# Cross-attention with a layer norm on one core: another order of all engines from the third tile on, and another ending for tiles 48 to 55

## The chip, the core and the metric

The kernel runs on one core of one Trainium2 chip. A core has a TensorE (PE in the profile) for matrix products, a VectorE (DVE), a ScalarE (ACT) and a GpSimd (POOL) for the rest, and a SyncE (SP) that issues most of the DMA transfers. Each engine runs its own instructions in order and waits on semaphores for the others. Matrix products are written to PSUM, eight banks of 128 x 512 floats; everything else lies in SBUF.

The metric is the device time of one execution, in microseconds. The times before are those of three runs.

## What is computed

Four sequences of 2048 rows attend to contexts of 77 rows, 512 features, 16 heads of 32. The projection is followed by a residual and a layer norm, everything in 32 bits:

```python
B, S, D, H = (2, 1024, 512, 16)
HD = D // H
qs = (q @ wq).reshape(Bq, Lq, H, HD).transpose(0, 2, 1, 3)
ks_ = (k @ wk).reshape(Bq, Lk, H, HD).transpose(0, 2, 1, 3)
vs = (v @ wv).reshape(Bq, Lk, H, HD).transpose(0, 2, 1, 3)
scores = jnp.einsum('bhqd,bhkd->bhqk', qs, ks_) / jnp.sqrt(jnp.float32(HD))
scores = jnp.where(mask[:, None, :, :], -jnp.inf, scores)
attn_w = jax.nn.softmax(scores, axis=-1)
attn = jnp.einsum('bhqk,bhkd->bhqd', attn_w, vs)
attn = attn.transpose(0, 2, 1, 3).reshape(Bq, Lq, H * HD)
out = attn @ wo + q
mu = jnp.mean(out, axis=-1, keepdims=True)
var = jnp.mean((out - mu) ** 2, axis=-1, keepdims=True)
return (out - mu) / jnp.sqrt(var + EPS) * gamma + beta
```

Here `q` is `x` (4 x 2048 x 512), and `k` and `v` are the context (4 x 77 x 512).

## The kernel before

The 8192 rows are 64 tiles of 128 rows. Two tiles make a pair (32 pairs, written b), four make a group (16 groups) for the query projection. A product of 32-bit numbers is made of three products of rounded parts: each operand is split into a high part and the rest (`xth` and `xtl`, `wqh` and `wql`, `AH` and `AL`, `woh` and `wol`).

The whole program is one string, `ORDER` (L49 to L143). Each of its words is one step: a letter for the kind, a number for the tile, pair or group, and sometimes a part. The loop at the end of `xattn_layernorm` issues the steps in the order of the string, and since a step's instructions go to the engine that its function names, the string sets the order in which each engine runs its work. A second table, `SLOTS`, says for every buffer of a kind, in the order in which they are asked for, which of the places it gets: `mm` for the eight banks of PSUM, `PT` and `B` for two buffers each, `o` for eight, and so on. A step waits until the place that it writes is free.

The steps of a tile t of pair b, with the letter that stands for each in `ORDER`:

- Query: `g` loads four features' blocks of `x` transposed (SP), `i` rounds them (ScalarE, L265), `j` takes the rest (GpSimd, L269), `Q` makes one of four query blocks of a group with 12 matmuls (L275), `q` copies it out of PSUM (VectorE, L289).
- Scores: `S`, 64 short matmuls into four banks (L399). `T` with a part 0 to 3 adds the mask, takes the row maxima of four heads and writes to one of three `pbuf` (VectorE, L416). `e` with a part is the exponential of four heads, with its sum (ScalarE, L431). `r` is the reciprocal of the sums (VectorE, L441), `n` the normalisation (GpSimd, L446); the last tile does both in halves, `h` and `m` (L452, L458).
- Regrouping: `t` transposes blocks of 32 x 32 (VectorE, L467) into `B`; twelve DMAs per pair, `P` (L478; `U` for the two tiles of the last pair), move the blocks into `PT`. Their last letter is the queue: `s` for SP, `a` for ScalarE, `g` for GpSimd.
- Values' product: `V` for a pair (32 matmuls, L492), `W` for a tile of the last pair. `a` and `b` (`c` and `d` there) round the result (ScalarE, L521) and take the rest (VectorE, L525).
- Output: `O` projects with 12 matmuls (L548). The residual is added in one of two ways. With `X`, TensorE puts `x` into the bank first, by a product with an identity matrix in 32 bits (L537), and `O` adds to it. Without it, `+` adds the rows of `x` on VectorE (L557). `x` is the load of those rows (L533).
- Ending: `s` takes the moments (VectorE, L568 and L569, or L596 and L598). Then there are two ways. In the first, for a pair, `v` makes the inverse deviation and the shift with four small instructions (GpSimd, L574 to L577), `k` scales (ScalarE, L583), `f` multiplies by gamma and adds beta (GpSimd, L587 and L588). In the second, for a single tile, `u` makes the inverse deviation with two small instructions (GpSimd, L602 and L603), `y` takes off the mean and multiplies by gamma (VectorE, L614), `z` multiplies by the inverse deviation and adds beta (VectorE, L617). `w` stores (SP, L591).

Before, tiles 0 to 47 end in the first way and tiles 48 to 63 in the second, and `LATE = 48` tells `s` which moments a tile needs. Eight tiles have their residual on TensorE: 49, 51, 54, 55, 57, 59, 62 and 63.

One wait is set by hand. Where the word behind `S` among TensorE's words is a `V`, the first matmul of the scores also waits for the twelve regroupings of that `V` (`early_waits`, L385).

The middle of the string repeats, pair after pair, on TensorE: scores of the even tile, the values' product of two pairs back, scores of the odd tile, two query blocks, two output tiles.

Of the kernel before, what the change touches and what calls it, by code (L numbers as in the profile page):

```python
# [8 lines left out]
F32 = mybir.dt.float32  # L9
# [8 lines left out]
P = 128  # L18
# [25 lines left out]
LATE = 48  # L44
# [4 lines left out]
ORDER = """  # L49
R1 R0 R3 E l0 l2 C2 C0 C1 C3 g5 M4.4 A0 M0.1 M12.4 A1 M1.3 A3 M8.4 K2 A2 H2 J3 p i3 g4 J1 K0 i2 S0 I2 j2 S1 T0.1  # L50
e0.1 T0.2 H0 T0.0 j3 e0.0 T1.0 T0.3 e0.2 T1.1 Q4 T1.2 e0.3 F0 T1.3 I0 e1.2 r0 n0 S2 q4 e1.0 S3 T2.3 T2.0 Q7 i5 T2.1
e1.3 F2 j5 T2.2 t0 e1.1 Q6 i4 F1 g7 r1 Y1 e2.0 F3 L1 n1 T3.2 Q5 x1 T3.1 e2.1 q6 T3.3 e3.3 j4 t1 B0 e3.2 T3.0 P0.4s
q7 x2 e2.3 q5 P0.7s S4 D0 P0.5s e3.0 S6 P0.10s T4.3 P0.0s G0 B2 e3.1 R2 T4.0 g6 P0.2s e4.3 r3 P0.8s G3 n3 P0.11s B1
e2.2 D2 P0.6s T4.1 T4.2 e4.1 G2 r2 Q8 i7 t3 x11 n2 P0.3s e4.2 P0.9s T6.0 P0.1s T6.2 e4.0 j7 x0 Q9 T6.3 Z13.s t2
e6.0 Z0.s G1 e6.3 S5 r4 P1.0s T6.1 n4 P1.7s q8 Q10 e6.2 T5.3 P1.6s T5.0 P1.10s e6.1 T5.2 P1.3s T5.1 P1.5s i6 S7 t4
P1.1s Z1.s e5.3 Q11 j6 P1.11s T7.2 P1.9s e7.2 T7.3 Z2.s q9 P1.8s r6 e7.3 D1 Q13 n6 P1.4s T7.0 P1.2s T7.1 e7.0 g9
q10 x3 e7.1 Z12.s V0 q13 g8 q11 Z11.s a0.0 r7 e5.0 t6 V1 Z10.s n7 Z7.s e5.1 b0.0 S9 N t7 a1.1 Q12 e5.2 b1.1 P3.9s
a1.0 P3.5s r5 T9.0 n5 P3.11s e9.0 Q14 b1.0 P3.3s T9.2 Z8.s e9.2 T9.1 P3.2s T9.3 P3.4s e9.3 t5 Y0 S8 P3.10s a0.1 O2
P3.7s q12 i9 T8.1 P3.0s T8.0 e9.1 P2.3s T8.3 P3.8s q14 Z9.s e8.0 O3 T8.2 P3.1s b0.1 P3.6s e8.3 +2 Z5.s r9 P2.0s n9
e8.2 S10 +3 P2.7s S11 P2.2s T10.0 e8.1 s2 P2.9s O1 j9 s3 T10.3 e10.3 r8 T10.1 v1 g10 Q15 +1 e10.1 Z4.s t9 n8 P2.6s  # L60
k2 x6 T10.2 P2.11s e10.0 V3 f2 t8 i8 T11.3 P4.11s O0 e11.3 T11.2 P2.4s j8 q15 P4.9s a3.0 T11.0 P2.8s k3 T11.1 P2.1s
a3.1 S12 w2 e10.2 M16.4 P2.5s b3.1 Q19 +0 P4.6s e11.1 r10 P4.5s T12.2 n10 P2.10s b3.0 e11.2 T12.0 P4.10s O6 s0
P4.7s i10 f3 P4.8s s1 P4.0s e11.0 q19 T12.3 S13 e12.2 t10 v0 w3 V2 P4.3s r11 x7 T13.2 a2.0 n11 e13.2 P4.1s T13.1 O7
# [110 lines left out]
def xattn_layernorm(  # L174
# [381 lines left out]
    def residual(t):  # L556
        nc.vector.tensor_tensor(od[t], pos.pop(t), od[t], ALU.add)  # L557
# [202 lines left out]
```

## Time and profile before

| What | us |
| --- | --- |
| Runs shown | 524.79, 529.14, 530.62 |
| Median of them | 529.14 |
| Span of the profiled execution | 525.7 |
| TensorE's clock granted in it, of full speed | 0.997 |

The profiled execution has no time of its own beside its span, which is from its first instruction to its last; it lies inside the runs' spread. The profile counts an engine as busy from the start to the end of each instruction. TensorE's matmuls overlap, so that a matmul of 512 columns is shown as some 0.39 us long while the next starts 0.23 us later; the time of a group of them is therefore read from the chain of work, which counts from start to start. A row of the groups of instructions has the line, the engine, the operation, what it writes and reads by the program's names, the form, the count, then the busy time in us and the mean of one in ns, and then the idle time ahead of them with what ended it. "issue" is time in which the engine waited for nothing that the profile shows.

### The profile page before, as it was taken

How to read it: one execution, taken by the hardware profiler on the slowest of the kernel's cores; microseconds unless marked ns; L12 is line 12 of the kernel's file. 1: busy time of each engine (PE TensorE's matmuls, PEld its weight loads, DVE VectorE, ACT ScalarE, POOL GpSimd, SP SyncE). 2: the span in 40 equal slices, each digit the busy share in tenths (PEclk: the TensorE clock that was granted, in tenths of full speed). 3: DMA queues.
4: the chain of work that ended last, by engine and by line, in shares of the span. 5: the costliest groups of instructions: out<-in, count | busy, mean ns of one | idle time of the engine just before them, and what ended most of it. 6: DMA issues, size and time to landing. Idle time of an engine off the chain costs nothing.

```text
span 525.7 us, 20274 instructions
## 1 busy us (share of the span) xinstructions
PE 507.2 (96%) x6845; PEld 388.8 (74%) x6845; DVE 476.0 (91%) x2572; ACT 460.4 (88%) x2215; POOL 405.5 (77%) x371
## 2 busy tenths in 40 slices
PE   9999999999989999999999999999999999999994
PEld 6987777778767777777777777767777777767662
DVE  5798988989979989998989989998998999999997
ACT  6699999998989999999999999999999999987400
POOL 2475736889889889969989887988888689869551
PEclk9999999999999999999999999999999999999998
DMA  8948577785797677988887687797868987388555
GB/s 300 401 125 241 148 205 196 195 236 147 205 243 226 189 197 225 217 219 219 215 225 207 178 224 226 184 254 195 213 190 225 259 251 189 91 219 218 158 176 199
DMA packets 59261, 110.85 MB, mean 211 GB/s; under 512 B 9430, under 2 KB 11758, under 8 KB 59158
## 3 DMA queue, kind: packets, MB, share of 16 engines
q1 hardware_dynamic: 55702, 102.75, 69.1%
q0 software_dynamic: 2496, 5.77, 3.9%
q10 hardware_dynamic: 960, 1.05, 0.8%
q8 instruction: 54, 0.88, 0.7%
q14 instruction: 49, 0.40, 0.3%
HBM read 41.79 MB, written 16.78 MB: 111 GB/s over the span
## 4 chain that ended last, share of the span: by engine, by line
PE 51%; DVE 12%; DMA 10%; POOL 9%; SPq 9%; ACT 5%; issue 3%; POOLq 0%; DVEq 0%
PE pq L275 20%; PE po L548 15%; PE sc L399 7%; SPq L478 6%; PE pa L492 6%; DMA PT<-B 6%; ACT pbuf L431 4%; POOL o L587 3%; DVE B L467 3%; POOL o L588 2%; POOL pbuf L446 2%; DVE pbuf L416 2%; PE pv L326 2%; DMA stage_a<-xT 1%; POOL xtl L269 1%
## 5 line engine op out<-in xcount | busy, mean ns | idle before, releaser
L431 ACT ACTIVATE pbuf<-pbuf,nm 128x77 f32<-128x77 f32 x1024 | 352.7, 350 | 16.2 <-DVE nm L416 13.4
L431 ACT ACTIVATION_READ_ACCUMULATOR pbuf<-pbuf,nm 128x1 f32 x1024 | 194.6, 190 | 0.0
L416 DVE CUSTOM_DVE_ANT_0 pbuf<-sc,mb 128x77 f32<-128x77 f32 x1024 | 170.2, 231 | 9.6 <-PE sc L399 8.5
L446 POOL TENSOR_TENSOR pbuf<-pbuf,ri 128x1232 f32<-128x1232 f32 x63 | 142.8, 2267 | 39.4 <-DVE ri L441 23.6
L467 DVE STREAM_TRANSPOSE B<-pbuf 128x1280 f32<-128x1280 f32 x64 | 96.1, 1502 | 9.8 <-POOL pbuf L446 5.4
L548 PE MATMUL po<-woh,AH 128*128 128x512 f32 x256 | 102.6, 401 | 0.0
L548 PE MATMUL po<-woh,AL 128*128 128x512 f32 x256 | 100.1, 391 | 2.3 <-DVE AL L525 2.3
L275 PE MATMUL pq<-xth,wqh 128*128 128x512 f32 (+1 forms) x256 | 101.8, 398 | 0.2
L548 PE MATMUL po<-wol,AH 128*128 128x512 f32 x256 | 99.8, 390 | 0.0
L275 PE MATMUL pq<-xtl,wqh 128*128 128x512 f32 (+1 forms) x256 | 98.3, 384 | 0.0
L275 PE MATMUL pq<-xth,wql 128*128 128x512 f32 (+1 forms) x256 | 98.1, 383 | 0.0
L416 DVE DVE_READ_ACCUMULATOR2_ANT nm<- 128x1 f32 x1024 | 83.9, 82 | 0.0
L399 PEld LDWEIGHTS sc<-kct,q 32*64 32x64 f32 x4096 | 52.8, 130 | 32.9 <-issue 17.1
L587 POOL TENSOR_TENSOR o<-o,gam 128x512 f32<-128x512 f32 x48 | 62.5, 1302 | 13.7 <-ACT o L583 13.4
L269 POOL TENSOR_TENSOR xtl<-xtf,xth 128x1024 fp32r<-128x1024 f32 x28 | 67.3, 2403 | 6.7 <-ACT xth L265 6.6
L399 PE MATMUL sc<-kct,q 32*64 32x77 f32 x4096 | 63.6, 238 | 8.4 <-issue 3.8
L588 POOL TENSOR_TENSOR o<-o,bet 128x512 f32<-128x512 f32 x48 | 62.4, 1300 | 3.8
L492 PE MATMUL pa<-PT,vsb 96*32 96x256 f32 x992 | 59.9, 382 | 0.0
L521 ACT CAST AH<-pa 128x512 fp32r<-128x512 f32 x64 | 36.4, 572 | 25.0 <-DVE st L596 10.6
L548 PEld LDWEIGHTS po<-woh,AL 128*128 128x128 f32 x256 | 48.0, 188 | 13.8 <-DVE AL L525 3.5
L548 PEld LDWEIGHTS po<-woh,AH 128*128 128x128 f32 x256 | 48.0, 188 | 13.7 <-issue 2.0
L275 PEld LDWEIGHTS pq<-xth,wqh 128*128 128x128 f32 x256 | 48.1, 188 | 12.0 <-PE sc L399 0.5
(108 smaller groups left out, 666.0 us busy)
## 6 DMA issues: line engine op xcount, KB each, us to landing
PT<-B SPq DMA_DIRECT2D x343, 128.0 KB
xtf<-xT SPq DMA_DIRECT2D x28, 512.0 KB
o<-x SPq DMA_DIRECT2D x56, 256.0 KB
out<-o SPq DMA_DIRECT2D x56, 256.0 KB
PT<-B POOLq DMA_DIRECT2D x25, 128.0 KB, 3.8
xtf<-xT SPq DMA_DIRECT2D x4, 256.0 KB
stage_a<-wq SPq DMA_DIRECT2D x4, 256.0 KB
stage_a<-wk SPq DMA_DIRECT2D x4, 256.0 KB
```

The source lines that it names most:

```text
L269: nc.gpsimd.tensor_tensor(l[:, c : c + 2], fx.pop((g, c)), xh[g][:, c : c + 2].bitcast(F32), ALU.subtract)
L275: nc.tensor.matmul(pq, w[:, c, m * P : (m + 1) * P], r[g][:, c, rs], start=(n == 0), stop=(n == 11))
L399: mm = nc.tensor.matmul(sc[j][r0 : r0 + SR, g * NK : (g + 1) * NK], qs[q, g, rs.start + r0 : rs.start + r0 + SR], kct[q, g, t // TPB, keys ...
L416: nc.vector.tensor_tensor_reduce(pb[:, h // 2, (h % 2) * NK : (h % 2 + 1) * NK], scs[t][j][:, g * NK : (g + 1) * NK], mb[:, t % TPB, keys_ ...
L431: nc.scalar.activation(pb[:, h // 2, (h % 2) * NK : (h % 2 + 1) * NK], pb[:, h // 2, (h % 2) * NK : (h % 2 + 1) * NK], AF.Exp, bias=nmax[t ...
L446: nc.gpsimd.tensor_tensor(pv, pv, rv.to_broadcast((P, NP, 2, NK)), ALU.mult)
L467: nc.vector.transpose(bt.rearrange("p c q r -> p q c r"), pbuf[t % NPB].rearrange("p q (c r) -> p q c r", c=5),)
L492: nc.tensor.matmul(pas[b, g // 2][HD * j : HD * (j + 1), (g % 2) * BLK : (g % 2 + 1) * BLK], vsb[:, 2 * b // TPB, h % 2, HD * (h // 2) : H ...
L521: nc.scalar.copy(*at_part(once(ahs, b, [P, NG, BLK], F32R, "AH"), b, i, by_tile))
L548: nc.tensor.matmul(pos[t], a[:, c, rs], w[:, c, :], start=(first and c == 0 and n == 0), stop=(c == NC_D - 1 and n == 2),)
L587: nc.gpsimd.tensor_tensor(o, o, gam, ALU.mult)
L588: nc.gpsimd.tensor_tensor(o, o, bet, ALU.add)
```

## The change

From the third tile on (behind the step `S5`) `ORDER` is another string, and the places of the banks and of the buffers `xtf`, `PT`, `AH`, `AL`, `o`, `mv` and `rn` follow it. Functions, formats and the number of places stay. Two things besides the order change:

- Pairs 24 to 27 (tiles 48 to 55) end in the first way: `v`, `k` and `f` take the place of `u`, `y` and `z`. Tiles 56 to 63 keep the second. Instead of `LATE`, a set `ALONE` is read off the string.
- Tiles 49, 51, 54, 55, 57 and 59 have their residual on VectorE, `+`, instead of `X`. Tiles 62 and 63 keep `X`.

Counted over the string, `X` goes from 8 words to 2, `+` from 56 to 62, `u`, `y` and `z` from 16 to 8 each, `v` from 24 to 28, `k` and `f` from 48 to 56 each. All other kinds of step keep their number.

The diff, with a few lines of the two strings from the place where they part (behind `S5`; the lines are also broken elsewhere) and from their ends:

```diff
-LATE = 48
 LAST = 56
...
-e6.0 Z0.s G1 e6.3 S5 r4 P1.0s T6.1 n4 P1.7s q8 Q10 e6.2 T5.3 P1.6s T5.0 P1.10s e6.1 T5.2 P1.3s T5.1 P1.5s i6 S7 t4
-P1.1s Z1.s e5.3 Q11 j6 P1.11s T7.2 P1.9s e7.2 T7.3 Z2.s q9 P1.8s r6 e7.3 D1 Q13 n6 P1.4s T7.0 P1.2s T7.1 e7.0 g9
...
+T4.1 T4.2 e4.1 G2 r2 Q8 i7 t3 x11 n2 P0.3s e4.2 P0.9s T6.0 P0.1s T6.2 e4.0 j7 x0 Q9 T6.3 Z13.s t2 e6.0 Z0.s G1 e6.3 S5
+Z12.s D1 q8 e6.2 i6 r4 T6.1 e6.1 Z2.s T5.0 e5.0 P1.3s P1.4s T5.1 Z11.s P1.7s q9 P1.6s P1.2s Q11 n4 t4 P1.0s S7 T7.1
+e7.2 e7.0 Q12 n6 t6 e5.3 r7 n7 S9 T9.2 e9.2 q12 r5 n5 T9.3 Z1.s V0 Y0 Z3.s g9 g8 T9.0 t7 P3.7s P3.5s P3.2s P3.4s V1
...
-U63.9a u59 y59 d62 z59 O62 z60 z57 z58 +61 z56 W63 s62 w56 c63 w51 X63 s61 u62 w57 d63 O63 u61 w58 y62 z55 y61 w55
-z62 z61 s63 w61 w59 u63 y63 w62 z63 w60 w63
+U62.3a U62.0a U62.4a W62 U63.1a y59 u58 v27 k55 k47 f53 U63.2s U63.11s W63 w53 y58 z57 w57 k54 f54 w54 +60 s60 z56 u60
+z59 z58 w58 w56 f55 w55 w59 c62 d62 O62 +61 s61 y60 u61 c63 d63 s62 u62 z60 y61 w60 w52 z61 w61 f47 w47 O63 s63 u63
+y62 z62 y63 w62 z63 w63
 """
+
+ALONE = {int(w[1:]) for w in ORDER.split() if w[0] in "u@"}
...
-        mvs[t, 1] = tiny.tile([P, 4], F32, tag="mvt", bufs=64 - LATE, name=f"mvt_{t}")
+        mvs[t, 1] = tiny.tile([P, 4], F32, tag="mvt", bufs=len(ALONE), name=f"mvt_{t}")
...
-        "+": lambda k, part: residual(k), "s": lambda k, part: (moments_one if k >= LATE else moments)(k),
+        "+": lambda k, part: residual(k), "s": lambda k, part: (moments_one if k in ALONE else moments)(k),
```

Three places show how the engines' rows move. In them a name carries the tile, pair or group and a buffer's number: `sc_38_3` is the fourth bank of tile 38's scores, `pa_16_0` half of pair 16's values' product, `PT_16` its regrouped weights, `po_31` the output of tile 31, `mvt_60` the moments of tile 60 and `o_55` the rows of tile 55.

The first place is TensorE around the values' product of pair 16, which reads the regrouped weights of tiles 32 and 33. Before, it stands between the scores of tiles 38 and 39:

```order
L399 MATMUL sc_38_2_5338<-kct_74,q_9_4717 64x77
L399 MATMUL sc_38_3_5339<-kct_74,q_9_4717 64x77
L492 MATMUL pa_16_0_5374<-PT_16_5047,vsb_75 32x256 x8
L492 MATMUL pa_16_1_5375<-PT_16_5047,vsb_75 32x256 x8
L399 MATMUL sc_39_0_5418<-kct_74,q_9_4717 64x77
L399 MATMUL sc_39_1_5419<-kct_74,q_9_4717 64x77
```

Now, the scores of tiles 39 and 40 stand ahead of it and an output of tile 31 behind it:

```order
L398 MATMUL sc_40_2_5489<-kct_74,q_10_5200 64x77
L398 MATMUL sc_40_3_5490<-kct_74,q_10_5200 64x77
L491 MATMUL pa_16_0_5523<-PT_16_4969,vsb_75 32x256 x8
L491 MATMUL pa_16_1_5524<-PT_16_4969,vsb_75 32x256 x8
L547 MATMUL po_31_5579<-woh_72,AH_15_5326 128x512
L547 MATMUL po_31_5579<-wol_73,AH_15_5326 128x512
```

So the product of pair 16 has moved back by two groups of scores, and the scores that also wait for its regroupings are those of tile 40 instead of 38.

The second place is SP's queue in the regrouping of pair 16. Before, its twelve transfers stand among two loads of rows, one of the transposed input and two stores:

```order
L478 DMA PT_16_5047<-B_16_4920 32x2x512
L533 DMA o_33_5051<-x 128x512
L262 DMA xtf_11_0_5056<-xT 128x1024
L478 DMA PT_16_5047<-B_16_4920 32x2x512 x2
L591 DMA out<-o_27_4239 128x512
L478 DMA PT_16_5047<-B_16_4920 32x2x512
L591 DMA out<-o_24_4167 128x512
L478 DMA PT_16_5047<-B_16_4920 32x2x512 x7
L533 DMA o_32_5253<-x 128x512
L478 DMA PT_16_5047<-B_16_4920 32x2x512
```

Now, there is one store among them, and the mask of the last sequence (a line's number is one less in the changed kernel):

```order
L477 DMA PT_16_4969<-B_16_4824 32x2x512 x4
L261 DMA xtf_11_0_4996<-xT 128x1024
L590 DMA out<-o_22_4216 128x512
L477 DMA PT_16_4969<-B_16_4824 32x2x512
L375 DMA m8_3_5012<-mask 128x1536
L477 DMA PT_16_4969<-B_16_4824 32x2x512
L532 DMA o_28_5093<-x 128x512
L477 DMA PT_16_4969<-B_16_4824 32x2x512 x2
L532 DMA o_32_5106<-x 128x512
L477 DMA PT_16_4969<-B_16_4824 32x2x512 x4
```

The regroupings stay in SP's queue among other transfers; which transfers those are, and how many stand together, has changed.

The third place is GpSimd's end. Before, its last twelve rows are three issues of the last pair's regroupings and the inverse deviations of the last tiles:

```order
L478 DMA PT_31_8834<-B_31_8778 32x2x256
L602 TENSOR_TENSOR mvt_60_8938<-mvt_60_8938,small_78 128x1
L603 TENSOR_TENSOR mvt_60_8938<-mvt_60_8938,small_78 128x1
L478 DMA PT_31_8834<-B_31_8778 32x2x256 x2
L602 TENSOR_TENSOR mvt_59_8963<-mvt_59_8963,small_78 128x1
L603 TENSOR_TENSOR mvt_59_8963<-mvt_59_8963,small_78 128x1
L602 TENSOR_TENSOR mvt_62_9032<-mvt_62_9032,small_78 128x1
L603 TENSOR_TENSOR mvt_62_9032<-mvt_62_9032,small_78 128x1
L602 TENSOR_TENSOR mvt_61_9041<-mvt_61_9041,small_78 128x1
L603 TENSOR_TENSOR mvt_61_9041<-mvt_61_9041,small_78 128x1
L602 TENSOR_TENSOR mvt_63_9070<-mvt_63_9070,small_78 128x1
L603 TENSOR_TENSOR mvt_63_9070<-mvt_63_9070,small_78 128x1
```

Now, the multiplications and additions of tiles 55 and 47 stand between the inverse deviations of tiles 60 to 63:

```order
L601 TENSOR_TENSOR mvt_60_9011<-mvt_60_9011,small_78 128x1
L602 TENSOR_TENSOR mvt_60_9011<-mvt_60_9011,small_78 128x1
L586 TENSOR_TENSOR o_55_8437<-o_55_8437,gam_76 128x512
L587 TENSOR_TENSOR o_55_8437<-o_55_8437,bet_77 128x512
L601 TENSOR_TENSOR mvt_61_9043<-mvt_61_9043,small_78 128x1
L602 TENSOR_TENSOR mvt_61_9043<-mvt_61_9043,small_78 128x1
L601 TENSOR_TENSOR mvt_62_9052<-mvt_62_9052,small_78 128x1
L602 TENSOR_TENSOR mvt_62_9052<-mvt_62_9052,small_78 128x1
L586 TENSOR_TENSOR o_47_7508<-o_47_7508,gam_76 128x512
L587 TENSOR_TENSOR o_47_7508<-o_47_7508,bet_77 128x512
L601 TENSOR_TENSOR mvt_63_9079<-mvt_63_9079,small_78 128x1
L602 TENSOR_TENSOR mvt_63_9079<-mvt_63_9079,small_78 128x1
```

The inverse deviation of the last tile has two rows of tile 47 just ahead of it, and the regroupings have moved further ahead.

More of the change, by code (lines that the diff above doesn't have):

```diff
@@ L59 @@
[L59 to L63, printed above, removed]
```

193 lines of the change are left out of this document (97 added, 96 removed).

## The prediction

> **What bounds the kernel now.** I read the page's totals first, then a table by stretches, then the chain of the work that ended last, then groups of instructions by form. The totals (engine, busy us, share of the span):
>
> ```profile
> PE 507.2 (96%) x6845; PEld 388.8 (74%) x6845; DVE 476.0 (91%) x2572; ACT 460.4 (88%) x2215; POOL 405.5 (77%) x371
> ```
>
> TensorE looks like the bound, with four engines close behind it. The stretches are cut at the starts of the scores of tiles 18, 54, 60 and 63:
>
> ```profile
> core 0: us, PE busy (x) PEld busy (x) DVE busy (x) ACT busy (x) POOL busy (x), PEclk, DMA share, GB/s
> 148.40:415.30 266.90, 261.80 (x3720) 202.27 (x3720) 243.28 (x1387) 255.03 (x1229) 231.80 (x192) 1.00 0.79 214
> 415.30:478.90 63.60, 62.66 (x893) 45.88 (x892) 61.34 (x367) 61.22 (x318) 50.83 (x52) 1.00 0.72 201
> 478.90:525.70 46.80, 38.23 (x341) 26.50 (x340) 43.08 (x102) 12.54 (x54) 23.83 (x43) 0.97 0.58 181
> 459.20:525.70 66.50, 56.99 (x617) 39.72 (x616) 62.32 (x217) 30.42 (x150) 39.34 (x57) 0.98 0.65 194
> ```
>
> There are two regimes. From 148 to 415 us TensorE is idle for 266.9 - 261.8 = 5.1 us; before 148 it is idle for 148.4 - (507.2 - 261.8 - 62.7 - 38.2) = 3.9 us, some of it at the start that stays as it is. I take 2 us of that as open to the change. After 415 VectorE is the fullest: 61.3 + 43.1 = 104.4 us of 110.4. The chain of the middle, where nothing waits (start, us, what):
>
> ```profile
> 283.70 0.88 PE sc L399 x53
> 284.58 1.86 PE pa L492 x32
> ...
> 293.01 5.44 PE po L548 x24
> 298.45 0.88 PE sc L399 x54
> 299.33 1.86 PE pa L492 x32
> ```
>
> A pair of tiles takes 298.45 - 283.70 = 14.75 us: two groups of scores, one values' product, two query and two output groups of 2.72. What costs time in between is this, in the same chain:
>
> ```profile
> 138.66 1.62 SPq L478
> ...
> 142.22 5.11 DMA PT<-B
> 147.33 1.10 issue
> 148.42 1.02 PE sc L399 x47
> ...
> 257.38 0.42 PE sc L399 x11
> ```
>
> The scores stand for 1.1 us and more behind regrouping DMAs: the first matmul of scores that stand right ahead of a values' product also takes over that product's wait. For pair 16, the scores of tile 33 end at 257.8 and its product starts at 299.33: 41.5 us. By the order, TensorE has 12 groups of 2.72, five scores of 0.88 and two products of 1.86 there, 40.8 us. So the path through the softmax, the transpose and twelve DMAs is about as long as TensorE's own work, and waits of a microsecond appear wherever it is a little longer. The end of the chain is VectorE, GpSimd and VectorE again, not TensorE:
>
> ```profile
> 519.32 0.75 DVE xtl L617
> 520.07 0.62 DVE st L596
> ...
> 521.83 0.75 DVE xtl L617
> ```
>
> **The new order in the middle.** It adds no work. Counted as above, the distance from a pair's last scores to its product is 40.8 us for each of pairs 8 to 23 before; now it is 43.4 on average, from 38.0 (pair 14) to 48.9. Pair 16 has 45.2 (13 groups, seven scores, two products); pair 17 has 38.9. On SP's queue the twelve regroupings still stand among five other transfers or so per pair, and stores still stand ahead of regroupings, so I cost that side at nothing beyond what the distance covers. Buffers placed anew cost nothing by themselves: the numbers of buffers stay. Bounds: a gain of 7 us if every wait that TensorE shows goes (5.1 + 2); a loss of 1 if those waits go and the path stays 41.5 us long, so that each short distance is paid (39.9 of pair 10, 38.0 and 38.9: 1.6 + 3.5 + 2.6 = 7.7); a loss of 8 if nothing else goes. I take -5, nearer the first, because 13 of 16 distances are as long or longer.
>
> **The end: tiles 48 to 55 and the residuals.** The durations, by form:
>
> ```profile
> L557 DVE TENSOR_TENSOR o<-po,o 128x512 f32<-128x512 f32 x52 | 35.0, 672 | 11.6 <-PE po L548 9.3 <-DMA o<-x 1.7 <-DMA PT<-B 0.5
> L614 DVE SCALAR_TENSOR_TENSOR o<-o,mvt,gam 128x512 f32<-128x512 f32 x4 | 4.2, 1062 | 0.0
> L614 DVE SCALAR_TENSOR_TENSOR o<-po,mvt,gam 128x512 f32<-128x512 f32 x4 | 2.9, 723 | 0.0
> L617 DVE SCALAR_TENSOR_TENSOR o<-o,mvt,bet 128x512 f32<-128x512 f32 x8 | 6.7, 842 | 0.1
> L583 ACT ACTIVATE o<-o,rn 128x512 f32<-128x512 f32 x48 | 37.9, 807 | 0.0
> L587 POOL TENSOR_TENSOR o<-o,gam 128x512 f32<-128x512 f32 x48 | 62.5, 1302 | 13.7 <-ACT o L583 13.4
> L588 POOL TENSOR_TENSOR o<-o,bet 128x512 f32<-128x512 f32 x48 | 62.4, 1300 | 3.8
> L575 POOL TENSOR_TENSOR rn<-rn,small 128x2 f32<-128x2 f32 x24 | 16.9, 703 | 1.9
> L576 POOL TENSOR_TENSOR rn<-mv,rn 128x2 f32<-128x2 f32 x24 | 4.7, 197 | 1.9
> L602 POOL TENSOR_TENSOR mvt<-mvt,small 128x1 f32<-128x1 f32 x16 | 3.6, 228 | 14.5 <-DVE mvt L598 14.4
> L603 POOL TENSOR_TENSOR mvt<-mvt,small 128x1 f32<-128x1 f32 x16 | 8.9, 556 | 1.3
> L446 POOL TENSOR_TENSOR pbuf<-pbuf,ri 128x1232 f32<-128x1232 f32 x63 | 142.8, 2267 | 39.4 <-DVE ri L441 23.6 <-DMA PT<-B 7.9 <-DVE nm L416 7.0
> ```
>
> - VectorE loses eight centrings and eight finishings, 4.2 + 2.9 + 6.7 = 13.8 us, and gains six residuals, 6 x 0.67 = 4.0: -9.8 us.
> - TensorE loses six residuals. The chain has one at 1.05 us:
>
> ```profile
> 428.49 1.05 PE po L537 x2
> ```
>
>   That is 6.3 us, hidden wherever VectorE, ScalarE or GpSimd sets the pace; if that cover goes it is a gain, never a cost.
> - ScalarE gains eight scalings, 8 x 0.81 = 6.5 us, mostly after its last exponentials, where it is busy for 12.5 of 46.8 us: nothing.
> - GpSimd gains eight multiplications and additions (8 x 2.60 = 20.8) and four pairs of inverse deviations (one step of 0.70 and three like L576's, 1.29, so 5.2), and loses eight single ones (8 x 0.78 = 6.3): +19.7 us.
>
> So VectorE stops being the fullest, and GpSimd is late next. Behind the scores of tile 60 it had 39.34 us of work. By the order, seven more multiply-adds stand there (18.2), three more pairs' inverses (3.9), one more normalisation (2.27), six fewer single inverses (-4.7) and one DMA issue fewer (-0.6): 58.5 us. Behind its last instruction come a centring and a finishing (1.5) and the store, 525.7 - 522.6 = 3.1: 63.1 us from those scores to the end, against 66.5 now, if GpSimd never waits. That is a gain of 3.4. From tile 54's to tile 63's scores ScalarE is busy for 61.22 of 63.6 us and keeps its work, which leaves 2.4 at most ahead of that. Together 5.8 is the best; the other end is a loss (below). I take -4, because the multiply-adds give GpSimd something to do where it now stands waiting (L602's 14.4 us), though it will not be without waits.
>
> The sum against the profiled execution: 525.7 - 5 - 4 = 516.7. The median of the runs shown, 529.14, lies 3.4 above that span, inside their spread of 5.8; I apply the difference to it: 520.1.
>
> **Rivals.**
>
> *TensorE paces the end as well.* If GpSimd hardly waits and its late multiply-adds overlap, the residuals' 6.3 us counts too. From tile 60's scores TensorE has 13 output groups, four scores, four products, two half products of about 1.0 and two residuals, 35.4 + 3.5 + 7.4 + 2 + 2.1 = 50.4, then the closing chain (moments 0.62, an inverse 0.78, then 1.5 and 3.1), 6.0: 56.4, 10 less than now. With the 7 of the middle: 512. Against it: GpSimd's 63.1.
>
> *The short distances are paid.* The middle then loses 7.7 - 7 = 0.7 instead of gaining 5, the end gains 4: 526. For it: the path is 41.5 us long where I measured it.
>
> *GpSimd and VectorE hold each other up.* This pair of answers shows it, GpSimd first:
>
> ```profile
> 454.21 1.45 POOL L587 TENSOR_TENSOR o<-o,gam 128x512 f32<-128x512 f32 x1 [1.12 <-ACT o L583]
> 455.74 1.63 POOL L588 TENSOR_TENSOR o<-o,bet 128x512 f32<-128x512 f32 x1
> ```
>
> ```profile
> 453.76 0.75 DVE L614 SCALAR_TENSOR_TENSOR o<-o,mvt,gam 128x512 f32<-128x512 f32 x1
> 454.61 1.60 DVE L617 SCALAR_TENSOR_TENSOR o<-o,mvt,bet 128x512 f32<-128x512 f32 x1
> ```
>
> A finishing took 1.60 instead of 0.75 while a multiply-add ran, whose halves took 0.15 and 0.33 too long. Eight centrings and eight finishings remain on VectorE, now beside seven multiply-adds: at 1062 - 723 = 0.34 each, 16 x 0.34 = 5.4 us, which eats the end's 4: 525. [...]
>
> *GpSimd's queue ends the kernel late (slower).* It runs in order, and behind tile 60's scores it now waits for this (engine, line, for whom: total, times, longest):
>
> ```profile
> POOL mvt L602 <- DVE mvt L598: 14.4, 4, 5.4
> POOL pbuf L458 <- DVE ri L452: 3.2, 1, 3.2
> POOL PT L478 <- DMA out<-o: 2.3, 1, 2.3
> POOL pbuf L446 <- DVE ri L441: 2.0, 2, 1.7
> ```
>
> If the last three and half of the first stay, 14.7 us, the end takes 63.1 + 14.7 = 77.8, 11.3 more than now; with the middle's -5 the whole is 535. It decides from 3.4 us of waiting on, and makes the kernel 1% slower from 3.4 + 5 + 5.3 = 13.7. What is queued behind a waiting GpSimd is the normalisation of tile 63's halves, hence the last transposes, DMAs and products.
>
> **How the numbers follow.** 1% (5.3 us) is about what a measurement of this kernel can tell from no change. My forecast, 520 (its own range 515 to 524), 0.38; TensorE paces it, 512, 0.17; short distances, 526, 0.18; mutual holding up, 525, 0.11; GpSimd late, 535, 0.16. Faster by over 1%: 0.38 + 0.17 = 0.55; within 1%: 0.29; slower: 0.16. The range goes from 509, a little under the rival at 512, to 533, so that it leaves out the late GpSimd and little else.
>
> **What would show it.** Right in the middle: TensorE's idle time between the scores of tiles 18 and 54 falls under 2 us, and the chain has fewer regrouping DMAs. Wrong: pairs 14 and 17 wait for theirs. Right at the end: VectorE's work behind tile 54's scores falls to about 95 us and GpSimd's rises by 20. Wrong: VectorE's finishings take over a microsecond on average, or the chain's last 40 us stand on GpSimd. What would upset all of it is a new wait ahead of tile 18.

## The result: 0.9% faster, and the profile after

| | kernel before | changed kernel |
|---|---|---|
| median, us (15 runs each, taken side by side) | 527.79 | 522.44 |
| lowest to highest, us | 523.90 to 530.62 | 520.56 to 526.84 |
| span of the profiled execution, us | 525.7 | 520.8 |

The ratio is 0.9912, with a 95% interval of 0.9886 to 0.9938. The forecast was 520, 1.7% faster; the direction came, with 5.35 us of the 9 forecast. By the ratio that is just inside the 1% that was called no change; by the medians it stands right at it.

The totals of the changed kernel (engine, busy us, share of the span) answer to the first line of the prediction:

```profile
PE 502.8 (97%) x6833; PEld 385.6 (74%) x6833; DVE 473.8 (91%) x2562; ACT 465.6 (89%) x2223; POOL 427.3 (82%) x387
```

TensorE lost 4.4 us of work, VectorE 2.2, and GpSimd gained 21.8. The stretches between the scores of tiles 18, 54, 63 and the end, and from tile 60's scores:

```profile
core 0: us, PE busy (x) PEld busy (x) DVE busy (x) ACT busy (x) POOL busy (x), PEclk, DMA share, GB/s
143.30:409.30 266.00, 263.86 (x3721) 201.42 (x3720) 248.56 (x1411) 260.34 (x1244) 239.80 (x198) 1.00 0.79 219
409.30:473.80 64.50, 62.41 (x904) 47.69 (x901) 57.61 (x346) 60.31 (x313) 56.40 (x61) 0.97 0.78 213
473.80:520.80 47.00, 36.41 (x337) 25.75 (x336) 42.23 (x96) 17.75 (x63) 40.51 (x51) 0.95 0.51 160
453.90:520.80 66.90, 54.22 (x609) 39.21 (x608) 58.45 (x206) 34.20 (x150) 55.95 (x67) 0.94 0.61 179
```

Read by these cuts, the last two stretches got longer (64.5 for 63.6, 47.0 for 46.8), and everything was gained ahead of them. The cuts deceive a little, because the two orders have not done the same work at the same scores. At two places they have, on TensorE: at the scores of tile 16 (the values' product of pair 5 is next in both) and at those of tile 55. There the tables can be compared. The kernel before:

```profile
132.10:421.80 289.70, 283.04 (x4017) 218.91 (x4016) 264.45 (x1522) 274.96 (x1328) 248.90 (x207) 1.00 0.79 216
421.80:525.70 103.90, 94.39 (x1145) 67.16 (x1144) 97.96 (x414) 67.82 (x339) 71.78 (x92) 0.98 0.64 186
```

The changed kernel:

```profile
131.30:418.60 287.30, 285.16 (x4017) 218.10 (x4017) 268.50 (x1525) 279.45 (x1335) 258.79 (x216) 1.00 0.78 216
418.60:520.80 102.20, 89.52 (x1133) 65.96 (x1132) 91.48 (x399) 68.76 (x331) 88.56 (x103) 0.96 0.67 192
```

- **Up to tile 16:** 0.8 us less (132.1 to 131.3).
- **From there to tile 55:** TensorE's idle time fell from 6.66 to 2.14 us. But its busy time rose by 2.1 us with the same 4017 products. Net 2.4 us less.
- **From tile 55 on:** TensorE has 12 products fewer in the count (the six residuals, which count as two each) and 4.9 us less busy time, and 3.2 us more idle time (12.7 for 9.5). Net 1.7 us less.

These are single executions, and the first two differences are no larger than what executions of the same order differ by. In ten traces that have the changed order up to tile 55 (the changed kernel's and those of runs below), the scores of tile 16 start between 130.7 and 132.0 us, and the way from there to tile 55 takes 286.6 to 287.6 us in nine and 289.5 in one (e_mid). The order before took 289.8 in the kernel before and 287.3 in e_end. What the middle is worth is therefore read from the runs (e_mid), not from these differences.

The 2.1 us of the middle are changeovers. In the starts of the products, between tiles 18 and 54, a group of 12 long products between two others takes 2.72 us from start to start; the first one behind scores or a values' product takes 2.84 to 2.87, the last ahead of them 2.81, one that is both 2.94. So each row of short products costs about 0.22 us. The order before has 20 such rows between tiles 16 and 55, the changed one 32: 12 x 0.22 = 2.6 us.

At the end, the wait of TensorE that stands out in the changed kernel is this one (start, busy, engine, line, operation, count; the bracket is the idle time ahead and what ended it):

```profile
456.13 0.61 PE L491 MATMUL pa<-PT,vsb 96*32 96x256 f32 x8
456.68 0.89 PE L398 MATMUL sc<-kct,q 32*64 32x77 f32 x56
459.65 0.36 PE L398 MATMUL sc<-kct,q 32*64 32x77 f32 x8 [2.08 <-issue]
...
461.97 0.63 PE L547 MATMUL po<-wol,AH 128*128 128x512 f32 x1
462.39 0.63 PE L547 MATMUL po<-woh,AL 128*128 128x512 f32 x1
```

It falls in the middle of tile 61's scores, and "issue" means that no semaphore explains it. Behind it, products start 0.43 us apart instead of 0.23: the granted clock halved. The window table of those stretches shows it (the column behind POOL is the granted clock):

```profile
457.30:459.65 2.35, 0.27 (x23) 0.10 (x11) 2.35 (x10) 2.35 (x15) 2.27 (x2) 1.00 0.93 242
461.28:464.69 3.41, 3.41 (x10) 2.63 (x9) 1.34 (x15) 0.72 (x2) 2.70 (x4) 0.51 0.73 212
```

Last, the finishing operations that stay on VectorE, by form:

```profile
L616 DVE SCALAR_TENSOR_TENSOR xth<-xth,mvt,bet 128x512 f32<-128x512 f32 x4 | 4.9, 1260 | 0.0
L616 DVE SCALAR_TENSOR_TENSOR xtl<-xtl,mvt,bet 128x512 f32<-128x512 f32 x4 | 3.7, 917 | 0.3
L613 DVE SCALAR_TENSOR_TENSOR xth<-xth,mvt,gam 128x512 f32<-128x512 f32 x4 | 2.9, 738 | 0.0
L613 DVE SCALAR_TENSOR_TENSOR xtl<-xtl,mvt,gam 128x512 f32<-128x512 f32 x2 | 2.4, 1198 | 0.0
L613 DVE SCALAR_TENSOR_TENSOR xtl<-po,mvt,gam 128x512 f32<-128x512 f32 x2 | 1.5, 729 | 0.0
```

The finishings take 8.6 / 8 = 1.08 us on average, not 0.75. The two centrings that read a bank of PSUM (po) are not slowed.

VectorE's total fell by no more than 2.2 us for a second reason too. Its fifteen large scalings of the mask, operations with one input, got longer by 3.9 us in all; before, then now:

```profile
L382 DVE TENSOR_SCALAR mb<-m 128x384 bf16<-128x384 uint8 x15 | 7.0, 468 | 0.0
L381 DVE TENSOR_SCALAR mb<-m 128x384 bf16<-128x384 uint8 x15 | 10.9, 728 | 0.0
```

With GpSimd idle one takes 0.30 to 0.36 us. At 177.3 us in the changed kernel one took 2.19, beside a normalisation of GpSimd that took its usual 2.26; the addition of a residual (L556) came behind it, and TensorE's scores of tile 23 waited 0.72 us for that.

### The profile page after: what moved, and what is told of

It reads as the page before. It is cut to its first block, busy times and chain, and to the rows that moved or that the text cites. A ratio compares the mean times of both kernels' runs of the same rounds, so it can differ in the third digit from the quotient of the medians.

```text
span 520.8 us, 20280 instructions
## 1 busy us (share of the span) xinstructions
PE 502.8 (97%) x6833; PEld 385.6 (74%) x6833; DVE 473.8 (91%) x2562; ACT 465.6 (89%) x2223; POOL 427.3 (82%) x387
## 4 chain that ended last, share of the span: by engine, by line
PE 69%; DVE 13%; DMA 6%; POOL 5%; SPq 3%; issue 2%; ACT 1%; ACTq 0%; DVEq 0%; POOLq 0%
PE po L547 25%; PE pq L274 25%; PE pa L491 9%; PE sc L398 8%; DVE pbuf L415 2%; DVE B L466 2%; SPq L477 2%; DMA PT<-B 2%; PE pk L297 1%; POOL pbuf L445 1%; POOL o L587 1%; POOL o L586 1%; DMA xtf<-xT 1%; DVE st L595 1%; ACT pbuf L430 1%
## 5 line engine op out<-in xcount | busy, mean ns | idle before, releaser
L430 ACT ACTIVATION_READ_ACCUMULATOR pbuf<-pbuf,nm 128x1 f32 x1024 | 198.0, 193 | 0.0
L547 PE MATMUL po<-woh,AH 128*128 128x512 f32 x256 | 104.1, 407 | 0.2 <-PE sc L398 0.2
L587 POOL TENSOR_TENSOR o<-o,bet 128x512 f32<-128x512 f32 x56 | 73.2, 1307 | 4.4
L586 POOL TENSOR_TENSOR o<-o,gam 128x512 f32<-128x512 f32 x56 | 73.1, 1305 | 3.3 <-ACT o L582 3.3
L398 PE MATMUL sc<-kct,q 32*64 32x77 f32 x4096 | 61.6, 238 | 3.0 <-issue 2.3
L547 PEld LDWEIGHTS po<-wol,AH 128*128 128x128 f32 x256 | 48.5, 190 | 9.8 <-issue 0.5
## 6 DMA issues: line engine op xcount, KB each, us to landing
xtf<-xT SPq DMA_DIRECT2D x28, 512.0 KB, 5.0
```

Source lines behind the costliest of these rows:

```text
L398: mm = nc.tensor.matmul(sc[j][r0 : r0 + SR, g * NK : (g + 1) * NK], qs[q, g, rs.start + r0 : rs.start + r0 + SR], kct[q, g, t // TPB, keys ...
L430: nc.scalar.activation(pb[:, h // 2, (h % 2) * NK : (h % 2 + 1) * NK], pb[:, h // 2, (h % 2) * NK : (h % 2 + 1) * NK], AF.Exp, bias=nmax[t ...
L547: nc.tensor.matmul(pos[t], a[:, c, rs], w[:, c, :], start=(first and c == 0 and n == 0), stop=(c == NC_D - 1 and n == 2),)
L586: nc.gpsimd.tensor_tensor(o, o, gam, ALU.mult)
L587: nc.gpsimd.tensor_tensor(o, o, bet, ALU.add)
```

## Experiments

My theory after the result: the order up to tile 55 brings 3 to 4 us, and of 3.3 us that the six residuals are worth on TensorE some 2 are given back behind the last scores. Each run below stood beside runs of the kernel before on the same chip; "against the changed kernel" is worked out from two ratios and good to about 0.5%. A kernel built anew has other line numbers (for instance L614 for L616).

**The order's first part alone (e_mid).** Words of the order up to S55 are the changed kernel's; behind it, what is left stands as in the kernel before, with X residuals and y, z endings for tiles 48 to 55:

```diff
-... S55 T55.1 w42 T55.2 T55.3 P25.10s t53 P25.7s V24 ...   (changed kernel)
+... S55 P25.3g e53.3 P25.7s M56.4 V24 T55.3 ... X49 ...    (kernel before)
```

> The order of the changed kernel up to the scores of tile 55, then what is left in the order of the kernel before, with its endings of tiles 48 to 55 and its six TensorE residuals. Theory 1 (from the two traces: the new order saves TensorE 3.3 us of waiting up to tile 54, and the rest of the 5.4 us is the residuals): 524 to 525 us where the kernel before takes 527.8, 3 to 4 us faster. The recorded sum: 5 us faster, 522.8. Theory 2 (the whole gain is the end): within 1 us of the kernel before.

Measured: 522.94 us, ratio 0.9909 (0.9876 to 0.9942). From tile 55 on, its profiled execution:

```profile
421.10:523.10 102.00, 93.37 (x1145) 66.81 (x1144) 95.23 (x409) 63.23 (x323) 66.08 (x87) 0.98 0.66 192
```

The first part alone gives the whole gain: the recorded sum for it was right, theory 1 expected 1 to 2 us less, and theory 2 is out. With the old end behind it the end takes 102.0 us, as with the new end (102.2). So the new endings and the six moved residuals together are worth nothing that can be measured here, which is to within some 2 us. The same old end took 103.9 us in the kernel before. Behind the new middle VectorE has 95.2 us of work left at tile 55 instead of 98.0, ScalarE 63.2 instead of 67.8 and GpSimd 66.1 instead of 71.8; a part of the middle's gain shows only behind tile 55. The profiled execution itself ran 2.5 us behind the changed kernel's at tile 55, though the order up to there is the same; the verdict rests on the runs.

**The order's second part alone (e_end, e_end2).** The kernel before up to S55 (e_end) or S52 (e_end2), then the changed order:

```diff
-... S52 T52.2 ... (order of the kernel before)
+... S52 ... (what is left, in the changed kernel's order and with its endings)
```

> The order of the kernel before up to the scores of tile 55, then what is left in the order and with the endings of the changed kernel. Theory 1 (six residuals are worth 3.3 us on TensorE, start to start 0.55 us each, and about 2 us of that is given back behind the last scores, where VectorE and GpSimd hold each other up): 525 to 527 us, 1 to 2.5 us faster than the kernel before. The recorded sum: 4 us faster, 523.8. Theory 2 (the whole gain is the end): 522.4, like the changed kernel.

> The order of the kernel before up to the scores of tile 52, then the order and the endings of the changed kernel; at this cut the two kernels have done the same TensorE work and differ by fewer instructions on the other engines than at the scores of tile 55, where VectorE's maxima of tile 55 came 4 us late behind the cut. Theory 1 (the end gives back what the residuals save): within 2.5 us of the kernel before, 525.5 to 528. The recorded sum, 4 us for the end: 524. If the end itself loses, as the first cut showed: 529 or more.

Measured: 530.50 us, ratio 1.0054 (1.0019 to 1.0090), and 531.16 us, 1.0063 (1.0033 to 1.0094). e_end is slower than every theory had it. e_end2 came out where the third of its recorded cases has it, "if the end itself loses", but the changed kernel loses nothing against e_mid, which has the old end, and neither run isolates the end. At the seam VectorE and ScalarE have not done what the order behind it counts on: in e_end TensorE lost 4.1 us ahead of the scores of tile 56 and 4.0, at half clock for the most part, in the two groups behind them; in e_end2 it lost 8 us between the scores of tiles 54 and 56, in four pieces. I take them as inconclusive for the end's worth. They do show that the new end needs what the new middle leaves done on the other engines: in both, the scores at the seam waited for VectorE.

**VectorE and GpSimd in each other's way (e_memset).**

```diff
     def affine(t):
+        if t == 47 or t >= 50:
+            for _ in range(5):
+                nc.gpsimd.memset(o, 0.0)
+            return
         nc.gpsimd.tensor_tensor(o, o, gam, ALU.mult)
```

> The changed kernel in which GpSimd's two multiply-adds of tiles 47 and 50 to 55 (2.6 us a tile) are replaced by five fills of the same tile (some 2.7 us by the fills of 0.21 us for 128 columns and 0.94 us for 1024), which read nothing; these tiles leave out the normalised values. Theory 1 (VectorE's operations with two SBUF inputs and GpSimd's hold each other up): y and z of tiles 58 to 62 at 0.75 us instead of up to 1.8 us, TensorE's wait ahead of the output product of tile 62 about 2 us shorter, 518 to 519.5 us, 3 to 4 us faster than the changed kernel. Rival (GpSimd's queue is simply full): y and z shorter or not, the time within 1 us of the changed kernel's 522.4.

Measured: 521.88 us, ratio 0.9893 (0.9835 to 0.9950); 0.2% against the changed kernel, which is nothing. Three finishings in a row, in the changed kernel, then in this one, and all sixteen operations of this one by form:

```profile
501.75 4.14 DVE L616 SCALAR_TENSOR_TENSOR xth<-xth,mvt,bet 128x512 f32<-128x512 f32 x3
```

```profile
501.44 2.04 DVE L614 SCALAR_TENSOR_TENSOR xth<-xth,mvt,bet 128x512 f32<-128x512 f32 x3
```

```profile
L614 DVE SCALAR_TENSOR_TENSOR xtl<-xtl,mvt,bet 128x512 f32<-128x512 f32 x4 | 3.0, 744 | 2.4 <-POOL mvt L600 2.3
L611 DVE SCALAR_TENSOR_TENSOR xth<-xth,mvt,gam 128x512 f32<-128x512 f32 x4 | 2.9, 739 | 0.0
L614 DVE SCALAR_TENSOR_TENSOR xth<-xth,mvt,bet 128x512 f32<-128x512 f32 x4 | 2.8, 740 | 0.0
L611 DVE SCALAR_TENSOR_TENSOR xtl<-xtl,mvt,gam 128x512 f32<-128x512 f32 x2 | 1.5, 736 | 0.0
L611 DVE SCALAR_TENSOR_TENSOR xtl<-po,mvt,gam 128x512 f32<-128x512 f32 x2 | 1.5, 732 | 0.0
```

Tiles 47 and 50 to 55 come out as zeros here. The mechanism is shown: with GpSimd only writing, every such operation takes 0.73 to 0.74 us, 3.7 us less in all (15.4 to 11.7 over the sixteen), and the last output product ends at 509.9 instead of 512.8. Of these 2.9 us, 1.4 are there already at the scores of tile 63 (472.4 for 473.8), because the clock stayed full behind the stall in tile 61's scores; the fills did not do that. Its price is not shown: VectorE now waits 2.3 us for GpSimd's inverse deviations (L600), which stand behind the fills in GpSimd's queue. From the last product to the last finishing it takes 6.3 us instead of 4.9, and the kernel gains 1. Both theories had half of it.

**What six residuals are worth on TensorE (e_pe6).**

```diff
         first = t not in pos
         if first:
             pos[t] = bank(f"po_{t}")
+        if t in (49, 51, 54, 55, 57, 59):
+            nc.tensor.matmul(pos[t], ident, od[t], start=True, stop=True)
```

> The changed kernel with six more TensorE products of the residual's size, one ahead of each of the output products of tiles 49, 51, 54, 55, 57 and 59, into the bank that the output product then overwrites; VectorE's adds stay. Theory 1 (TensorE paces the stretch and each costs it 0.55 us from start to start): 3 us slower than the changed kernel, 525.5 us. The length of 1.05 us in the profile's groups would give 6 us, 528.5. Rival (the end is set by VectorE and GpSimd): no change, 522.4.

Measured: 529.63 us, ratio 1.0034 (1.0004 to 1.0064): 1.0034 / 0.9912 = 1.2% slower than the changed kernel, 6.4 us, give or take 2. From tile 55 on:

```profile
417.50:526.60 109.10, 94.69 (x1145) 68.44 (x1144) 93.16 (x400) 69.18 (x333) 89.08 (x103) 0.96 0.62 180
```

109.1 us for 102.2: 5.2 us more of TensorE's work (94.7 for 89.5) and 1.7 of idle time, of which 1.1 is the stall in tile 61's scores, 3.19 us long here instead of 2.08. So in the new end TensorE's work counts in full, and the rival (no change) is out. One such product costs 0.86 us of it; the start-to-start time of 0.46 to 0.56 was too low a price, since the first product behind it takes 0.64 us to the next start instead of 0.23.

**The residuals without the endings (e_resid).** e_mid with the six X taken out and VectorE's additions put ahead of the moments:

```diff
-X49 ... s49 ... X51 ... s51 ... X55 ... X54 ...
+... +49 s49 ... +51 s51 ... +55 s55 ... +54 s54 ...
```

> The run e_mid with one more change: the six TensorE residuals (tiles 49, 51, 54, 55, 57, 59) are additions on VectorE, as in the changed kernel, while tiles 48 to 55 stay ended by VectorE. Theory 1 (TensorE paces the end, as six products put into the changed kernel cost 6 us, and it is the endings on ScalarE and GpSimd that give this back): 3 to 6 us below e_mid, 516 to 520 us where the kernel before takes 528. Rival (VectorE, which gets six additions of 0.67 us, paces the end in this order): e_mid's time or up to 4 us above it, 523 to 527.

Measured: 527.73 us, ratio 1.0019 (0.9989 to 1.0048): 1.1% slower than e_mid. The rival had the way and the cause right, and the size a little too low (up to 4 us; the medians are 4.8 apart). The stretch from tile 55, and what TensorE waited for in it (for whom: total, times, longest):

```profile
418.20:525.90 107.70, 92.68 (x1133) 66.25 (x1132) 101.11 (x422) 64.64 (x331) 67.03 (x87) 0.97 0.63 182
```

```profile
PE po L541 <- DVE AL L518: 5.6, 7, 1.7
PE sc L392 <- DVE nm L409: 2.1, 2, 1.8
```

VectorE was the fullest there and now has 101 us of work in 107.7; TensorE waits for its splits (AL) and maxima (nm). So the residuals moved alone cost 1.1%, with the additions standing where they do here. The changed kernel against e_resid (0.9912 / 1.0019) brings 1.1% back, by the moved endings and the new order of the end together; which of the two, no run tells. In all: nothing, as e_mid said.

**The last split earlier on VectorE (e_order).**

```diff
-... z59 z58 w58 w56 f55 w55 w59 c62 d62 O62 +61 s61 y60 u61 c63 d63 s62 ...
+... z59 c62 d62 c63 d63 z58 w58 w56 f55 w55 w59 O62 +61 s61 y60 u61 s62 ...
```

> The changed kernel with ScalarE's and VectorE's split of the attention rows of tiles 62 and 63 (c, d) ahead of VectorE's last operation of tile 58; nothing else moves. Theory 1 (VectorE has no gap from 497 us on, and what it does is only handed round): TensorE's wait of 1.9 us ahead of tile 63's output product goes, and the time stays within 1 us of the changed kernel, 522. Rival (the path runs through that wait of TensorE): 2 us faster than the changed kernel, 520.5.

Measured: 523.07 us, ratio 0.9914 (0.9886 to 0.9942), the changed kernel's to a hair, as theory 1 had it. The last output product ended at 509.6 instead of 512.8, and the last finishing at 517.7, as in the changed kernel: VectorE does the same work in another order, and tile 47's multiply-adds still stand ahead of the last tile's inverse in GpSimd's queue.

**Tiles 54 and 55 back on VectorE (e_half).**

```diff
-v27 k55 k47 f53 U63.2s U63.11s ... k54 f54 w54 ... f55 w55 ... f47 w47
+y54 z54 w54 u55 ... y55 ... k47 f53 f47 w47 U63.2s U63.11s ... z55 w55
```

> The changed kernel with tiles 54 and 55 ended by VectorE again (four operations of 0.75 us there; 2 x 2.6 + 2.4 us less on GpSimd), the last multiply-adds of tile 47 right behind tile 53's, and the split of tiles 62 and 63 early as in e_order. Theory 1 (GpSimd's last microseconds and VectorE's stretched operations are one cost, both from the late multiply-adds): 2 to 4 us faster than the changed kernel, 518.5 to 520.5. Rival (VectorE is full in the end, so 3 us more there count): 522 to 525.

Measured: 528.33 us, ratio 1.0011 (0.9973 to 1.0049), 1% slower than the changed kernel and outside both expectations. I had built a flaw into it. SP's queue from 507 us on, and TensorE's longest wait:

```profile
507.19 0.34 SPq L584 DMA_DIRECT2D out<-o  x1
507.58 1.23 SPq L471 DMA_DIRECT2D PT<-B  x2
```

```profile
PE pa L500 <- DMA PT<-B: 5.6, 1, 5.6
```

The store of tile 47 stood ahead of the last pair's two regroupings and waited for GpSimd; the regroupings went out at 507.6 instead of 494.8, and the last half product waited 5.6 us. That wait is about the size of the 1%. Whether the two tiles are better on VectorE stays open.

**A long group between the short ones (e_fetch).**

```diff
-... V27 ... n59 t59 P29.2s P29.6s S61 T61.2 f49 e60.2 e60.1 T61.0 e60.3 T61.3 O50 +50 ...
+... V27 ... n59 t59 P29.2s P29.6s O50 S61 T61.2 f49 e60.2 e60.1 T61.0 e60.3 T61.3 +50 ...
```

(the banks behind it placed anew)

> The changed kernel with TensorE's output product of tile 50 (12 products, 2.7 us) between the values' product of pair 27 and the scores of tile 61, which the changed kernel runs in a row with the scores of tile 60: 160 short products with their weight loads in 3.7 us, behind which TensorE stands 2.31 us in the middle of tile 61's scores with no releaser in the profile, 1.4 us longer than a 16 KB instruction packet in the trace, and then has 3.41 us at clock 0.5. Theory 1 (the stall is the fetch of TensorE's instructions, drained by the row of short ones): the stall under 1 us, no 3.41 us at half clock there, the scores of tile 63 start 2 to 3.5 us earlier than in the changed kernel; the time 519 to 521, since GpSimd and VectorE at the end take part of it. Rival (the stall is a wait for a bank or for VectorE): the stall stays over 2 us, and the time at the changed kernel's 522.4.

Measured: 520.82 us, ratio 0.9866 (0.9822 to 0.9910), 0.5% below the changed kernel. The same stretch of TensorE:

```profile
459.47 0.39 PE L541 MATMUL po<-woh,AL 128*128 128x512 f32 x1
459.79 0.95 PE L392 MATMUL sc<-kct,q 32*64 32x77 f32 x64
460.67 0.50 PE L541 MATMUL po<-woh,AH 128*128 128x512 f32 x1
```

```profile
417.80:518.20 100.40, 89.83 (x1133) 66.14 (x1132) 92.85 (x409) 70.27 (x340) 89.42 (x103) 0.97 0.67 194
```

The scores of tile 61 run through, the clock stays full there, and the scores of tile 63 start at 470.1 instead of 473.8. Of these 3.7 us, 0.8 were there at tile 55 already; the end keeps 2.6 in all (last finishing at 515.1 for 517.7), 1.8 of them from behind tile 55. So the stall and the half clock behind it were made by the new order, and one word in another place takes them away.

The rival (a bank or VectorE) is out, and the kept traces speak strongly for a fetch of instructions. Seven of them have this row of 160 short products. In each TensorE stops at the same matmul of tile 61's scores, behind the 56th of 64 (in e_pe6, which has more products ahead, behind the 53rd), and goes on a nearly fixed time after a 16 KB instruction packet has landed, however long the stall is:

| run | stall, us | packet landed at | TensorE goes on at | between |
|---|---|---|---|---|
| e_end | 0.55 | 466.77 | 468.25 | 1.48 |
| e_memset | 1.87 | 458.31 | 459.91 | 1.60 |
| e_half | 1.94 | 459.03 | 460.46 | 1.43 |
| changed kernel | 2.08 | 458.20 | 459.65 | 1.45 |
| e_order | 2.29 | 457.68 | 459.10 | 1.42 |
| e_end2 | 2.63 | 469.29 | 470.73 | 1.44 |
| e_pe6 | 3.19 | 460.19 | 461.57 | 1.38 |

In e_fetch the packet lands at 458.30, while TensorE runs the long group. The kernel before has the same kind of stall in the middle of the scores of tiles 33 and 45 (and a third, of 0.27 us, in those of tile 51):

```profile
257.38 0.42 PE L399 MATMUL sc<-kct,q 32*64 32x77 f32 x18 [0.90 <-issue]
348.82 0.37 PE L399 MATMUL sc<-kct,q 32*64 32x77 f32 x10 [1.05 <-issue]
```

They end 1.59 and 1.49 us behind such a packet (the third 1.27). What no run did is to hold up a packet by itself. The order before has twenty rows of scores, product and scores, and only some of them stall.

**Three more moves at the end (e_best, e_last).** e_best puts tile 47's scaling behind e60.3, its multiply-adds ahead of n60 and its store ahead of w50, and takes e_order in. e_last goes further:

```diff
-... +57 ... +59 s59 u59 V30 a30.0 s58 b30.0 X62 y57 a30.1 b30.1 O60 ...
+... X57 O57 ... X59 O59 ... V30 a30.0 a30.1 b30.0 b30.1 y56 ... s59 u59 s58 X62 y57 O60 ...
```

> e_fetch, and three moves for the end: tile 47's scaling and multiply-adds ahead of GpSimd's normalisation of tile 60, where ScalarE and GpSimd stand idle for 3.1 and 2.6 us, its store ahead of tile 50's, and the split of tiles 62 and 63 early as in e_order. Theory 1 (GpSimd's queue and the stretched operations of VectorE set the last microseconds): 3 to 5 us below the changed kernel, 517.5 to 519.5. Rival (VectorE alone is full behind tile 63's scores): no more than e_fetch.

> e_best with VectorE's split of pair 30's attention rows (b) ahead of its work on tiles 56, 58 and 59, and two of the six residuals (tiles 57 and 59) back on TensorE, 1.05 us each there and 0.67 us less on VectorE. In e_best TensorE stood 4.2 us in the output product of tile 60, waiting for that split, with 3.41 us at half clock behind it. Theory 1 (VectorE's order and load behind tile 63's scores set the end): that wait under 1 us, no half clock before the last output product, the last output product done 1 to 3 us earlier than e_best's 511.5, the time 518 to 520.5. Rival (VectorE's total and GpSimd's late multiply-adds set the end whatever the order): within 1 us of e_best, 521 to 523.

Measured: e_best 522.16 us, ratio 0.9889 (0.9852 to 0.9927); e_last 521.46 us, 0.9874 (0.9835 to 0.9914). Neither beats e_fetch, and both miss the time that theory 1 gave them. By its time the rival of e_last was right. In e_best the output product of tile 60 took 4.2 us too long, first waiting for VectorE, then at half clock; the rival was right that VectorE gives out. In e_last that loss is 0.3 us and the half clock is gone; the last product ends at 509.9 instead of 511.5, within the expectation, and the last finishing only 0.9 earlier, at 516.6, since tile 61's waits for its inverse deviation until 512.0, behind tile 55's multiply-adds on GpSimd.

**The waits of the scores in the kernel before (b_noearly).**

```diff
-                    if first:
-                        early_waits(mm, t)
```

> The kernel before with one rule out: scores that stand just ahead of a values' product no longer take over that product's wait for its regrouping transfers; the product waits itself. Recorded reading of the middle (the gaps of TensorE ahead of scores are waits for those transfers): the scores run in the gaps, each of the seven gaps of 0.9 to 2 us ahead of scores between tiles 18 and 52 loses up to 0.88 us, 2 to 5 us faster than the kernel before. Rival (the gaps are waits for banks or maxima): within 1 us.

Measured: 525.59 us, ratio 0.9947 (0.9916 to 0.9978): 2.8 us faster, inside the forecast of 2 to 5. The gaps ahead of scores in the kernel before are, for a part of that size, waits for regrouping transfers that the scores themselves do not need. Not all of the gaps are of this kind: four stand ahead of the first matmul of scores (tiles 18, 28, 40 and 52: 1.58, 0.64, 1.27 and 0.76 us), which alone takes over such a wait, and in this run's profiled execution they are gone. The stall in the middle of tile 45's scores is still there, with 1.67 us.

## Why the prediction was half right

- **The middle, -5: near in size, right in mechanism for a part.** e_mid, which has only this, measured 0.9% (0.6 to 1.2), 4.8 us, and removing the regrouping waits by another way (b_noearly) was worth 2.8 us. Two things were wrong in it. First, "it adds no work": more changeovers between short and long products give back 2.1 us. Second, every wait of TensorE was put down to the regrouping transfers. Of the 5.1 us between tiles 18 and 54 (the wait of tile 18 itself lies just ahead of them), 2.7 stand ahead of a first matmul and 2.2 in the middle of the scores of tiles 33, 45 and 51, where nothing regrouped is waited for; the row at 257.38 that the prediction shows as such a wait is one of these. The new order lost both kinds, the second unforeseen. The sign named, idle time under 2 us between the scores of tiles 18 and 54, came out at 2.1.
- **Short distances: did not show.** Pairs 14 and 17, with 38.0 and 38.9 us, have no gap over 0.2 us of TensorE ahead of them. The path of 41.5 us had been measured on one pair with a wait in it, and was not a floor.
- **The end, -4: this is the term that failed.** It measured 0 (e_mid against the changed kernel, 0.9909 and 0.9912). VectorE's load fell by half of what was forecast (behind tile 54's scores 99.8 us for 104.4, where 95 was forecast; 3.7 of the missing 4.8 are stretched operations), and GpSimd's rose by 22 for 20. But two of the sum's steps went wrong:
  - The residuals were credited with nothing on TensorE, "hidden wherever VectorE, ScalarE or GpSimd sets the pace". In the old end that is so (e_resid: moving them alone makes it 1.1% slower). In the new end it is not: there products of their size cost 5 to 6 us (e_pe6). The rival "TensorE paces the end as well" had this half.
  - The gain of 4 was taken from the loads, as if waits stayed what they were. New ones came: the stall in tile 61's scores with half clock behind it (worth 2.4 us in the time, e_fetch, with an interval that reaches to nothing), and a close of 4.9 us behind the last output product for 3.2 before, where tile 47's multiply-adds stand ahead of the last inverse.
- **The two engines holding each other up: right as a mechanism, wrong as a price.** The finishings were over a microsecond, the sign that was named, and by forms 3.7 us were lost for 5.4 forecast. Taken away, this gave 1 us of time, less than the measurement can tell from nothing, since GpSimd's queue stood next. Beside the fills, which only write, the centrings and finishings took 0.73 to 0.74 us by form, and in the changed kernel the two centrings that read PSUM took 0.73, one of them beside a multiply-add (0.72, at 513.9 us). The scalings of the mask, with one input, did get longer (0.35 us alone, 2.19 beside a normalisation). In the finishings both sides got longer: three took 4.14 us instead of 2.04, and a multiply-add beside them 3.4 instead of 2.6.
- **GpSimd late: not as the bound of the kernel.** Waits of 14.7 us did not come; GpSimd is busy for 40.5 of the last 47 us. It holds up the last finishings by 1 to 2 us, no more, and the chain's last 30 us stand on VectorE.
- **Some luck in the number.** The forecast of 520 started from 529.14, the median of three runs; the median of fifteen is 527.79. So 522.44 lies 2.4 us from the forecast, where the gain itself came 3.7 short of it.

What stays open is whether this is all of the 5 to 6 us that the end gives back. The stall with half clock (2.4), the slower close (1.7) and the stretched operations (1 by itself) make 5.1 if they added up; that they add was not tried, and e_best and e_last, which took away several of them at once, ended above e_fetch.

The fastest version found is e_fetch: 0.9866 against the kernel before. Its interval overlaps the changed kernel's.

## What to carry to other kernels

When four engines are as busy as here (82 to 97% of the span), a load moved from one to another is worth nothing until the next one's waits are counted: six residuals taken off TensorE cost 1.1% in one order of the end, and six products of their size put back cost 1.2% in another. Compare two orders only at places where the same work is done; cutting at the same tile's scores gave 5.1 us to the part ahead of tile 18 here, where 0.8 at tile 16 is what equal work shows, and even that is no more than executions of one order differ by. And when a new order mixes short and long products more finely, count the changeovers and look for stalls that no semaphore ends: here they ended 1.3 to 1.6 us behind an instruction packet.

## What the hardware showed beside it

- A wait of TensorE of about 2 us can cost twice. Behind the one of 2.08 us in tile 61's scores the granted clock fell to 0.5 for 3.41 us, 1.7 us after the wait's end; from tile 55's scores to tile 63's it took 55.2 us, and 53.6 in e_memset, where a wait of 1.87 us left the clock full. The wait's length alone does not decide: the clock fell behind 1.78 us in e_resid and stayed behind 1.94 in e_half. Where it lies does more. In every trace any two changes of the clock lie whole multiples of 3.413 us apart (134, 1 and 15 in the changed kernel, in order of time, and 151 in the kernel before), so that the clock changes on a grid of its own. On this grid, the changed kernel's wait lies in one window, and that of e_memset in two:

```profile
457.93:461.34 3.41, 1.69 (x14) 1.36 (x14) 3.41 (x23) 2.95 (x18) 3.25 (x4) 1.00 0.50 134
```

```profile
455.60:459.01 3.41, 2.44 (x88) 1.44 (x81) 3.41 (x28) 3.34 (x20) 3.33 (x2) 1.00 1.07 278
459.01:462.42 3.41, 2.51 (x18) 2.04 (x18) 3.41 (x28) 2.27 (x14) 3.33 (x3) 1.00 0.36 90
```

TensorE is idle for 1.72 us of the first and for 0.97 and 0.90 of the two others. From 60 us to the last product, in all fourteen traces, the ten windows with 1.70 us or more of idle time were followed by one at half clock, none with 1.45 or less was, and of the seven between four were. In the changed kernel the window of 1.72 us is the only one over 0.86; in the kernel before, the longest idle time in a window is 1.33 us, and the clock stayed full behind it.
- A change between short products and those with 512 columns cost TensorE about 0.22 us here for each row of short ones: in the changed kernel a group of 12 long products took 2.84 to 2.87 us behind such a row and 2.81 ahead of one, for 2.72 between two other groups.
- VectorE's and GpSimd's operations stretched each other in both directions: three finishings took 4.14 us instead of 2.04, and a multiply-add beside them 3.4 us instead of 2.6. A scaling of the mask on VectorE, with one input, took up to 2.19 us instead of 0.35, beside a normalisation of GpSimd that was not stretched (2.26 us, as on average).
- In the rows of short products TensorE stopped at stalls that no semaphore ends and went on 1.3 to 1.6 us behind the landing of a 16 KB instruction packet.
